# Layer 0 with both sequences sorted by expert, and layer 1's experts with their inner rows as 128 and 48, two blocks at a time

## The chip, the core and the metric

The kernel runs on one core of one Trainium2 chip. A core has a matrix engine (TensorE, PE in the profile, with its weight loads as PEld), a vector engine (VectorE, DVE), a scalar engine (ScalarE, ACT), a general engine (GpSimd, POOL) and SyncE (SP), which only issues transfers (DMA). Matrix results land in PSUM, which has eight banks of 128 x 512 floats; everything else lies in SBUF, in 128 partitions, or in the chip's main memory (DRAM in the code). The metric is the device time of one execution in microseconds, as the median of several runs. A profiled execution gives the trace that is read here.

## The reference

Two layers over x, 2 sequences of 1024 tokens with 128 floats each. Cut to what matters:

```python
for attn, ffn in ((L0_attn, L0_ffn), (L1_attn, L1_ffn)):
    xn = layernorm(x)
    x = x + attn(xn) + ffn(xn)

def L0_attn(x):      # 16 heads of 8, causal; q, k, v are x with signs
    return where(causal, sigmoid(4 * scale * q @ k.T), 0) @ v

def L0_ffn(x):       # 32 experts, inner width 64; each token takes 4
    cw = softmax(x @ gw + gb), kept for the best 4 in the best 4 of 8 groups
    y = sum over e of cw[:, e] * ((silu(x @ w1[e] + b1[e]) * (x @ w3[e] + b3[e])) @ w2[e] + b2[e])
    return y + (silu(x @ sw1 + sb1) * (x @ sw3 + sb3)) @ sw2 + sb2

def L1_attn(x):      # 16 heads of 8, softmax over all keys, with relative positions
    return softmax((q @ k.T + position term) * scale) @ v @ Wproj.T

def L1_ffn(x):       # 16 experts, inner width 176; each token takes 4; a shared expert of width 352
    w = sigmoid(x @ gate_w.T), the best 4 in the best 2 of 4 groups, normalised
    return sum over e of w[:, e] * ((silu(x @ gate[e].T) * (x @ up[e].T)) @ down[e].T) + shared(x)
```

## The kernel before, in words

**Order of work.** Only PE's order is written by hand: a table (`at(c, f, ...)`, L1319 on) says what is issued beside which attention step `c`, in three places of a step (before the scores, between scores and values, after the values), and a loop (L1444 to L1458) walks it. The other engines get their order from a scheduler that follows the program and the data; SP and POOL issue transfers in that order, one behind the other.

**Layer 0's attention** has 96 steps, 48 for each sequence (`steps0`, L714): one slice of four heads, one half of the queries (512), one tile of 128 keys. The order of the loops before is sequence, slice, half of the queries, key tile. `scores0` (L717) makes four matmuls (L731) into two double banks, two sigmoids on ACT (L737) and, where the key tile lies on the diagonal, a mask on POOL (L743). `values0` of the step before (L758) makes four more, into one bank that it adds up over the key tiles. Four of the eight key tiles of the second half, and all four of the first, lie on the diagonal, where the matmuls are 512, 384, 256 and 128 wide. Steps 0 to 47 are sequence 0.

**Layer 0's experts, sequence 0,** are dense: every token goes through all 32 experts. A unit is two experts (their inner widths of 64 side by side) and 512 tokens; `open_unit` issues two matmuls (L362, L363), a sigmoid (L375), two operations on DVE (L376, L377) and the weighting by the gate (L379, on POOL or DVE, with rows that L360 broadcasts by DMA), and `close_unit` adds one matmul (L391) into a bank. The 32 units are spread over steps 13 to 51 of the attention. The weights lie in SBUF whole (L116 to L121).

**Layer 0's experts, sequence 1,** are sorted. `gate0` (L449) picks four experts for each token, `counted0` (L537) counts with two matmuls, `sort0` (L547) works out on DVE in which slot each choice goes, so that each expert's tokens fill blocks of 128 slots, and `scatter0` (L611) writes the normalised rows to their slots by 32 indirect transfers on POOL. The 64 blocks are taken in quads: `fetch0` (L626) gets four blocks of rows and their weights through SP, `turn0` (L643) transposes them (L647), `hidden0` (L651) makes 16 matmuls (L659), `outputs0` (L669) four in two groups (L675) and stores the result. A quad is due every one and a half steps from step 57. Then `gather0` (L683) brings each token's four rows back, by 32 indirect transfers on POOL, and `gathered0` (L693) adds them on DVE. `clear0` (L427) fills the slots with zeros and `regroup0` (L416) writes the weights in the order that `fetch0` reads; both are DMAs alone. The shared expert of both sequences, and that of layer 1 (`blocks1`), go by units as well.

**Layer 1** scans maxima of the scores (L1184 on PE; L1204, L1209 on DVE) ahead of a softmax attention of 128 steps (L1245 scores, L1252 exponentials on ACT, L1264 values), and uses a buffer of relative positions (`rel`, L1139) up to the last of the transfers that spread them. At step 67 `experts` (L1007) stands in PE's order by itself: 79 blocks of 128 slots, of both sequences, sorted in the same way. `fetch_w` (L934) fetches one block's weights, 128 rows of `WX` = 608 floats (two halves of 88 columns of gate and of up, two of down with 40 rows of zeros), into a ring of six places; `fetch_x` (L951) fetches four blocks of rows; `turn_x` (L967) transposes them; `hidden` (L979) makes four matmuls for a block (L984), one sigmoid (L987) and two multiplications (L988, L989); `outputs` (L992) two matmuls for the block of two turns before (L999), and a store for every four blocks (L1003). Of the weights, four blocks are fetched ahead, two steps before the stage.

## Time and profile before

| what | us |
|---|---|
| median of 3 runs (1292.96 to 1298.01) | 1293.78 |
| the profiled execution | 1295.13 |
| its span in the trace | 1293.0 |
| first scores of sequence 0, layer 0 | 12.61 |
| first scores of sequence 1, layer 0 (step 48) | 226.14 |
| quads of sequence 1 | 254 to 361.8 |
| last values of layer 0's attention | 436 |
| first exponentials of layer 1 | 511 |
| layer 1's experts | 867.5 to 995.2 |

The mean granted clock of the core's PE was 0.956 of full speed. PE was busy for 1161.0 us of the span with 8781 matmuls, the DMA engines moved 204.77 MB. Where a row of the profile names a line, it is a line of the kernel as printed above; `out<-in` are the names of its tiles, the shape is partitions x elements (for PE: weights, then result), and behind a bar stand the busy time with the mean of one in ns, and then the engine's idle time just ahead of these instructions with what ended most of it. The row of digits called PEclk is the clock that PE was granted, in tenths, over 40 equal slices of the span; DMA is the mean busy share of the 16 DMA engines.

### The profile page before, as it was taken

The numbers are of one execution on the slowest core, as the hardware profiler recorded it, in microseconds if no ns is written. First come the engines' busy times: TensorE is split into PE (matmuls) and PEld (weight loads), VectorE is DVE, ScalarE is ACT, GpSimd is POOL, SyncE is SP. The second block draws the span as 40 slices with busy tenths as digits, with TensorE's granted clock in tenths as the row PEclk, the third lists the DMA queues.
The fourth block names the chain that finished last, engine by engine and source line by source line (L and its number), as shares of the span: only waits on it lengthen the run. The fifth ranks groups of instructions, "written<-read, shape, count | busy, mean of one in ns | idle before, by whom it ended". The sixth has DMA issues, their size and how long they took to land.

```text
span 1293.0 us, 24010 instructions
## 1 busy us (share of the span) xinstructions
PE 1161.0 (90%) x8781; PEld 577.1 (45%) x8781; DVE 782.9 (61%) x2420; ACT 613.0 (47%) x1102; POOL 370.4 (29%) x475
## 2 busy tenths in 40 slices
PE   5989899989989777897999999988999999998997
...
PEclk8999999998999867899999999999999999998998
DMA  6955843445233331363356645579996454563511
GB/s 186 238 152 156 259 126 110 133 128 149 85 93 122 111 106 49 98 196 99 125 170 211 208 138 169 188 229 281 288 287 201 138 185 158 174 216 120 174 50 29
DMA packets 196313, 204.77 MB, mean 158 GB/s; under 512 B 26436, under 2 KB 178244, under 8 KB 196196
## 3 DMA queue, kind: packets, MB, share of 16 engines
...
## 4 chain that ended last, share of the span: by engine, by line
PE 63%; DVE 19%; DMA 8%; issue 5%; ACT 3%; POOL 2%; SPq 0%; POOLq 0%; DVEq 0%; ACTq 0%
PE sm L1245 11%; PE sm L1184 8%; PE acc L1264 8%; PE sm L1235 5%; PE big L731 4%; PE acc L758 4%; PE sm L984 4%; DVE maxima L1209 3%; PE big L362 3%; DVE junk L1204 3%; PE sm L1135 3%; PE big L363 2%; DMA got<-slots_y,slot_of 2%; PE ffn L391 2%; DMA room<-wx 2%
## 5 line engine op out<-in xcount | busy, mean ns | idle before, releaser
L1252 ACT ACTIVATE p<-sm 128x512 f32<-128x512 f32 x512 | 264.8, 605 | 231.3 <-PE sm L1245 224.2
L1209 DVE TENSOR_REDUCE maxima<-sm 128x1 f32<-128x512 f32 (+3 forms) x472 | 226.8, 502 | 101.6 <-PE sm L1184 101.6
L737 ACT ACTIVATE at<-big 128x1024 f32<-128x1024 f32 (+1 forms) x192 | 144.9, 809 | 139.4 <-PE big L731 134.1
L1204 DVE CUSTOM_DVE_ANT_0 junk<-sm,near 128x384 f32<-128x384 f32 (+2 forms) x292 | 130.3, 446 | 64.3 <-PE sm L1184 63.9
L1264 PE MATMUL acc<-p,vs 128*32 128x512 f32 (+1 forms) x1288 | 145.2, 520 | 0.4 <-issue 0.4
L1235 PE MATMUL sm<-ident,near 128*128 128x128 f32 x704 | 109.8, 290 | 25.9 <-DVE maxima L1204 11.2
L731 PE MATMUL big<-qm,xT 32*128 32x512 f32 (+3 forms) x768 | 109.5, 556 | 7.6 <-DVE qm L724 3.8
L1235 PEld LDWEIGHTS sm<-ident,near 128*128 128x128 f32 x704 | 79.7, 145 | 80.5 <-ACT p L1252 35.4
L1245 PE MATMUL sm<-qa,kls 32*128 32x512 f32 (+3 forms) x832 | 112.3, 556 | 0.0
L1184 PE MATMUL sm<-kls,qs 32*128 32x512 f32 (+2 forms) x776 | 105.8, 572 | 6.7 <-POOL kls L1116 5.4
L910 POOL DMA_INDIRECT got<-slots_y,slot_of x64 | 64.9, 1014 | 163.1 <-ACT p L1252 152.6
L758 PE MATMUL acc<-at,xn 128*32 128x512 f32 (+3 forms) x768 | 86.8, 526 | 8.3 <-DVE attn L343 5.3
L743 POOL TENSOR_SCALAR_AFFINE_SELECT at<-at 128x512 f32<-128x512 f32 x64 | 41.8, 654 | 179.8 <-ACT at L737 175.9
L898 POOL DMA_INDIRECT slots_x<-xn,slot_of x64 | 62.4, 976 | 94.6 <-ACT p L1252 84.8
L1139 ACT COPY rel<-sm 128x512 f32<-128x512 f32 x112 | 57.5, 599 | 61.5 <-PE sm L1135 61.5
L920 POOL TENSOR_SCALAR got<-got,share 128x128 f32<-128x128 f32 x64 | 41.4, 646 | 113.4 <-DMA got<-slots_y,slot_of 113.0
L1264 PEld LDWEIGHTS acc<-p,vs 128*32 128x32 f32 x1288 | 26.5, 108 | 103.7 <-issue 94.8
L1184 PEld LDWEIGHTS sm<-kls,qs 32*128 32x128 f32 x776 | 36.5, 186 | 80.8 <-ACT p L1252 21.1
L731 PEld LDWEIGHTS big<-qm,xT 32*128 32x128 f32 x768 | 40.6, 190 | 66.3 <-issue 41.2
L1135 PE MATMUL sm<-posd,qs 32*128 32x256 f32 x448 | 58.1, 422 | 11.9 <-DVE maxima L1209 10.9
L1116 POOL TENSOR_SCALAR khs<-kf,not_aux,k_add 128x1024 f32<-128x1024 f32 x8 | 9.6, 1195 | 187.7 <-PE sm L1245 187.7
L1245 PE MATMUL sm<-qa,khs 32*128 32x512 f32 (+3 forms) x512 | 60.9, 509 | 0.0
...
## 6 DMA issues: line engine op xcount, KB each, us to landing
...
```

The lines of the kernel that those rows point to most:

```text
L731: nc.tensor.matmul(halves[r // 2][:, r % 2, off:TB], xT0[b][g, kt * P:(kt + 1) * P], masked[b, s][g, q * TB + off:(q + 1) * TB], start=Tru ...
L737: e = nc.scalar.activation(at[:, 2 * j:2 * j + 2, off:TB], sc[:, :, off:TB], AF.Sigmoid, scale=4.0 / math.sqrt(HD))
L758: nc.tensor.matmul(y[32 * r:32 * r + 32, off:TB], xn0[b][:, kt * P + 32 * r:kt * P + 32 * r + 32], at[:, r, off:TB], start=(kt == 0), stop ...
L910: d = nc.gpsimd.indirect_dma_start(y, None, slots_y[:, :], bass.IndirectOffsetOnAxis(ap=slot_of[:, t, j:j + 1], axis=0))
L1135: nc.tensor.matmul(ps[r][:, j, :], qs[g, t:t + P], posd[g, :], start=True, stop=True)
L1184: nc.tensor.matmul(ps[r][:, (k0 - lo) * P:(k1 - lo) * P], qs[g, qt * P:(qt + 1) * P], (kh if far else kl)[g, k0 * P:k1 * P], start=True, s ...
L1204: nc.vector.tensor_tensor_reduce(junk[:, 0:(k1 - k0) * P], part, near[n, i][:, r, w0:w0 + (k1 - k0) * P], 1.0, -BIG, ALU.add, ALU.max, mx[ ...
L1209: nc.vector.tensor_reduce(mx[:, r, slot:slot + 1], part, AX.X, ALU.max)
L1235: nc.tensor.matmul(ps[r][:, i * P:(i + 1) * P], near[n, i][:, r, w0:w0 + P], ident, is_transpose=True, start=(i == close[0]), stop=False, ...
L1245: nc.tensor.matmul(ps[r][:, i0 * P:i1 * P], k[g, kt * P:(kt + 1) * P], qa[n][g, i0 * P:i1 * P], start=(m == 0 and not close), stop=(m == l ...
L1252: e = nc.scalar.activation(p[:, r, :], ps[r], AF.Exp)
L1264: nc.tensor.matmul(y[rows_of(r), part], vs[:, kt, rows_of(r)], probs[n, kt][:, r, part], start=(kt == 0), stop=(kt == NT - 1 and part.stop ...
```

## The change

Layer 0: sequence 0 loses its dense units and takes the sorted way too, with the same functions (now with the sequence as an argument, called from a new function `way0`). `sort0` counts and ranks by 27 small matmuls for each sequence, into the `ffn` bank, in place of the additions on DVE. Within a quad the slots are numbered so that each partition's four rows lie side by side in memory (2 KB for a transfer instead of four times 512 bytes); the slot's number is worked out by bit operations. The attention's loops run sequence, half of the queries, slice, key tile. Sequence 0's scatters stand at steps 25 to 42 and its quads, one a step, at 47 to 62; sequence 1's scatters at 46 to 58 and its quads at 63 to 78; the gathers at 64 to 76 and 81 to 93. The weights of a quad have a ring of five, the rows one of three.

Layer 1: a block's weights are 128 rows of 496 floats (gate, the last 64 columns of up, the first 128 of up, the first 128 rows of down) and 48 rows of 128 floats (the rest of down) by a second transfer, which goes into the tile of the relative positions. A block takes three matmuls and two in place of four and two, and ACT and DVE work for two blocks at once (two sigmoids, four multiplications). The ring of weights has 12 places, of which eight are fetched one step before the stage. The rows of four blocks are laid out like the quads. Smaller: layernorm's iteration takes three operations instead of four; the second half of sequence 1's rows is turned for layer 1 behind the first scan instead of ahead of it; layer 1's shared units and the clears and regroups stand at other steps.

```diff
-I1H = I1 // 2
-WX = 4 * I1H + 2 * D
+I1R = I1 - P
+IU = I1 + I0
+WX = IU + P + D
...
-    w1, w3 = ([load(l0, f"{n}{i}", [P, E0 * I0 // 2], a[n][:, i * E0 * I0 // 2:(i + 1) * E0 * I0 // 2])
-               for i in range(2)] for n in ("w1", "w3"))
...
+        nc.vector.tensor_scalar(var[:, c], var[:, c], -0.5, None, ALU.mult)
         for _ in range(3):
             nc.vector.tensor_mul(t[:, c], rstd[:, c], rstd[:, c])
             nc.vector.tensor_mul(t[:, c], t[:, c], var[:, c])
-            nc.vector.tensor_scalar(t[:, c], t[:, c], -0.5, 1.5, ALU.mult, ALU.add)
-            nc.vector.tensor_mul(rstd[:, c], rstd[:, c], t[:, c])
+            nc.vector.scalar_tensor_tensor(rstd[:, c], t[:, c], 1.5, rstd[:, c], ALU.add, ALU.mult)
...
-        if b == 0:
-            rest = l0.tile([P, NT, E0 + 4], F32, tag="rest", name="rest")
-            nc.vector.memset(work[:, :, E0:], NOT)
-            yield from replaced4(work, best, rest)
-            cw = cw_of[b] = l0.tile([P, NT, E0], F32, tag="cw", name="cw")
-            nc.vector.scalar_tensor_tensor(cw, rest[:, :, 0:E0], GONE, sc, ALU.is_equal, ALU.mult)
-            return
...
+    def sort0(b):
+
+        ps = psum["ffn"].tile([P, TB], F32, tag="ffn", name="counts")
+        n_at = NT * E0
+        at = ps[:, 0:n_at]
         some = some0.rearrange("p t e -> p (t e)")
-        for i, m in enumerate((ahead, ones)):
-            nc.tensor.matmul(ps[:, i * NT * E0:(i + 1) * NT * E0], m, some, start=True, stop=True)
-        counted[b] = [l0.tile([P, NT, E0], F32, tag=n, name="counted") for n in ("sc", "work")]
-        for i, t in enumerate(counted[b]):
-            nc.vector.tensor_copy(t.rearrange("p t e -> p (t e)"), ps[:, i * NT * E0:(i + 1) * NT * E0])
-
-    def sort0(b):
-
+        col = l0.tile([E0, 2], F32, tag="sort_col", name="sort_col")
+        full = l0.tile([E0, NT], F32, tag="sort_full", name="sort_full")
+        n_blk = l0.tile([E0, 1], F32, tag="sort_blk", name="sort_blk")
+        wide = l0.tile([E0, P], F32, tag="work", name="sort_wide")
+        past = l0.tile([E0, NBLK0], F32, tag="sc", name="sort_past")
+
+        for t in range(NT):
+            nc.tensor.matmul(ps[0:E0, n_at:n_at + 1], some0[:, t, :], ones[:, 0:1], start=(t == 0), stop=(t == NT - 1))
+
+        nc.tensor.matmul(at, ahead, some, start=True, stop=False, skip_group_check=True)
+        for t in range(1, NT):
+            nc.tensor.matmul(at[:, t * E0:], ones, some[:, 0:n_at - t * E0], start=False, stop=False,
+                             skip_group_check=True)
+        nc.vector.tensor_copy(col[:, 0:1], ps[0:E0, n_at:n_at + 1])
+        nc.vector.tensor_scalar(full, filled[0:E0, 0:NT], col[:, 0:1], None, ALU.is_lt)
+        nc.vector.tensor_reduce(n_blk, full, AX.X, ALU.add)
+        nc.vector.tensor_scalar(wide, ones[0:E0, :], n_blk, None, ALU.mult)
         yield
-        rank, in_tile = counted[b]
-        at = l0.tile([P, NT, E0], F32, tag="rest", name="at0")
-        count = [l0.tile([P, E0], F32, tag=f"count{i}", name=f"count{i}") for i in range(4)]
-        n_tok, n_blk = count[0], count[1]
-        nc.vector.memset(at[:, 0, :], 0.0)
-        for t in range(1, NT):
-            nc.vector.tensor_add(at[:, t, :], at[:, t - 1, :], in_tile[:, t - 1, :])
-        nc.vector.tensor_add(n_tok, at[:, NT - 1, :], in_tile[:, NT - 1, :])
+
+        for t in range(NT):
+            nc.tensor.matmul(at[:, t * E0:(t + 1) * E0], wide, before, start=False, stop=(t == NT - 1),
+                             skip_group_check=True)
+        nc.tensor.matmul(ps[0:E0, n_at + 4:n_at + 5], upto, n_blk, start=True, stop=True)
+        nc.vector.tensor_copy(col[:, 1:2], ps[0:E0, n_at + 4:n_at + 5])
+        nc.vector.tensor_scalar(past, block_no[0:E0, 0:NBLK0], col[:, 1:2], None, ALU.is_ge)
         yield
-        nc.vector.tensor_add(at, at, rank)
-        full = some0.rearrange("p t e -> p (t e)").rearrange("p (e t) -> p e t", t=NT)
-        nc.vector.tensor_tensor(full, spread(n_tok, NT), filled[:, 0:NT].unsqueeze(1).to_broadcast([P, E0, NT]),
-                                ALU.is_gt)
-        nc.vector.tensor_reduce(n_blk, full, AX.X, ALU.add)
-        yield
-
-        end, d = n_blk, 1
-        while d < E0:
-            nxt = count[2 + (d in (2, 8))]
-            nc.vector.tensor_add(nxt[:, d:], end[:, d:], end[:, 0:E0 - d])
-            nc.vector.tensor_copy(nxt[:, 0:d], end[:, 0:d])
-            end, d = nxt, 2 * d
-        yield
-        first = count[0]
-        nc.vector.tensor_sub(first, end, n_blk)
-        nc.vector.tensor_scalar(first, first, float(P), None, ALU.mult)
-        nc.vector.tensor_tensor(at, at, first.unsqueeze(1).to_broadcast([P, NT, E0]), ALU.add)
-        yield
+        nc.tensor.matmul(ps[:, n_at + 8:n_at + 8 + NBLK0], ones[0:E0, :], past, start=True, stop=True)
         slot = l0.tile([P, NT, K0], F32, tag="slot0f", name="slot0f")
         for j in range(K0):
-            nc.vector.tensor_mul(some0, chosen0[j], at)
+            nc.vector.tensor_mul(some, chosen0[j].rearrange("p t e -> p (t e)"), at)
             nc.vector.tensor_reduce(slot[:, :, j], some0, AX.X, ALU.add)
-            yield
-        nc.vector.tensor_copy(slot0, slot)
+            if j % 2:
+                yield
...
+        s0, lo, hi = (l0.tile([P, NT, K0], U32, tag=n, name="slot0i") for n in ("index0", "drop", "best0"))
+        nc.vector.tensor_copy(s0, slot)
+        nc.vector.tensor_scalar(lo, s0, P - 1, 2, ALU.bitwise_and, ALU.logical_shift_left)
+        nc.vector.tensor_scalar(hi, s0, 7, 3, ALU.logical_shift_right, ALU.bitwise_and)
+        nc.vector.tensor_scalar(s0, s0, 9, 9, ALU.logical_shift_right, ALU.logical_shift_left)
+        nc.vector.tensor_tensor(lo, lo, hi, ALU.bitwise_or)
+        nc.vector.tensor_tensor(slot0[b], s0, lo, ALU.bitwise_or)
...
+        w = l0.tile([P, 4, 2 * P], F32, tag="bw0", name="bw0", bufs=5)
...
+        x = l0.tile([P, 4, P], F32, tag="bx0", name="bx0", bufs=3)
+        d = nc.sync.dma_start(x, of_quad(slots0_x[b], g))
...
+        x = (x2s[b] if (b, t // 4) in merged else xs[b])[:, t, :]
...
+        parts = [(P, sw1, sw3, sw2, sb1, sb3)]
...
-    steps0 = [(b, s, q, kt) for b in range(B) for s in range(NS) for q in range(NB)
+    steps0 = [(b, s, q, kt) for b in range(B) for q in range(NB) for s in range(NS)
               for kt in range(4 * (q + 1))]
...
+    def of_four(slots, g):
+        return slots[4 * g * P:4 * (g + 1) * P, :].rearrange("(p i) d -> p i d", p=P)
...
+        if i == 0:
+            nc.sync.dma_start(by_row[:, :, 0:I1], gate)
+        elif i == 1:
+            nc.sync.dma_start(by_row[:, :, I1:IU], up[:, :, I1 - I0:])
+            nc.sync.dma_start(by_row[:, :, IU:IU + P], up[:, :, 0:P])
+        elif i == 2:
+            nc.sync.dma_start(wx.rearrange("(e p) w -> e p w", p=P)[:, :, IU + P:], down[:, 0:P, :])
         else:
-            c = slice(2 * I1 + (i - 2) * D, 2 * I1 + (i - 1) * D)
-            nc.sync.dma_start(wx.rearrange("(e p) w -> e p w", p=P)[:, 0:I1H, c],
-                              a["dproj"].rearrange("(e j p) d -> j e p d", j=2, p=I1H)[i - 2])
-            nc.sync.dma_start(by_row[I1H:P, :, c], zeros[I1H:P].unsqueeze(1).to_broadcast([P - I1H, E1, D]))
+            nc.sync.dma_start(wd.rearrange("(e p) d -> e p d", p=P)[:, 0:I1R, :], down[:, P:, :])
...
+    RING = 12
...
+        k = i % RING
+        if k < 8:
+            if k % 2 == 0:
+                held[k // 2] = const.tile([P, T], F32, tag=("xn10", "xn11", "xT10", "xT11")[k // 2], name="blockw")
+            t = held[k // 2]
         else:
-            t = held["p"][i % 2][:, 0:T]
+            t = held["p"][k // 2 % 2]
+        t = t[:, k % 2 * WX:(k % 2 + 1) * WX]
...
+        row = first_row.pop(i)
+        nc.sync.dma_start(t, wx[bass.ds(row, P), :])
+        rest = held["rel"][I0:I0 + I1R, k * P:(k + 1) * P]
+        nc.sync.dma_start(rest, wd[bass.ds(row, I1R), :])
+        block_w[i] = t, rest
...
+    def hidden(j):
+
+
+        n = min(2, NBLK - 2 * j)
+        ps, ps2 = quads(small()), quads(small())[:, 0:n, :]
+        for k in range(n):
+            i = 2 * j + k
+            w, xT = block_w[i][0], block_xT[i // 4][:, i % 4, :]
+            for m in range(2):
+                nc.tensor.matmul(ps[:, 2 * m + k, :], w[:, m * IU:m * IU + P], xT, start=True, stop=True)
+            nc.tensor.matmul(ps2[0:I0 + I1R, k, :], w[:, P:IU], xT, start=True, stop=True)
+        h = pools["late"].tile([P, 2, P], F32, tag="bh", name="bh", bufs=3)[:, 0:n, :]
+        c = RING * P + 2 * P * (j % 4)
+        h2 = held["rel"][:, c:c + 2 * P].rearrange("p (k c) -> p k c", c=P)[:, 0:n, :]
+        g2, u2 = slice(0, I1R), slice(I0, I0 + I1R)
+        nc.scalar.activation(h, ps[:, 0:n, :], AF.Sigmoid)
+        nc.scalar.activation(h2[g2], ps2[g2], AF.Sigmoid)
+        nc.vector.tensor_mul(h, ps[:, 0:n, :], h)
+        nc.vector.tensor_mul(h, ps[:, 2:2 + n, :], h)
+        nc.vector.tensor_mul(h2[u2], ps2[g2], h2[g2])
+        nc.vector.tensor_mul(h2[u2], ps2[u2], h2[u2])
+        block_h[j] = h, h2[u2]
...
+            ps, (w, rest) = block_y[g][:, i % 4, :], block_w.pop(i)
+            nc.tensor.matmul(ps, h[:, k, :], w[:, IU + P:], start=True, stop=False)
+            nc.tensor.matmul(ps, h2[:, k, :], rest, start=False, stop=True)
...
+        for i in range(8, RING):
             fetch_w(i)
-        for i in range(NBLK + 2):
-            if i < NBLK:
-                hidden(i)
-            if i >= 2:
-                outputs(i - 2)
-                fetch_w(i + 4)
-            if i % 4 == 1:
-                turn_x(i // 4 + 1)
-                fetch_x(i // 4 + 2)
+        for j in range(N_PAIRS + 2):
+            if j < N_PAIRS:
+                hidden(j)
+            if j >= 2:
+                outputs(j - 2)
+                for k in range(2):
+                    fetch_w(2 * (j - 2) + RING + k)
+            if j % 2 == 0:
+                turn_x(j // 2 + 1)
+                fetch_x(j // 2 + 3)
...
+    def way0(b, gate, per, sort, scatter, rate, quads_at, back, back_rate):
+
+        every(gate, gate0(b), per)
+        order = sort0(b)
+        for c in (sort, sort + 2, sort + 3, sort + 4, sort + 4, sort + 5):
+            at(c, one_part, order, slot=MID)
+        at(sort + 7, biased0, b, slot=END)
+        for i in range(NT * K0):
+            at(scatter + int(i / rate), scatter0, b, i, slot=END)
+            at(back + int(i / back_rate), gather0, b, i, slot=END)
+            at(back + 2 + int(i / back_rate), gathered0, b, i, slot=END)
+        for g in range(NQ0):
+            c = quads_at + g
+            at(c, hidden0, b, g, slot=MID)
+            at(c + 1, outputs0, b, g, slot=END)
+            at(c - 1, turn0, b, g, slot=END)
+        for g in range(NQ0):
+            at(quads_at + g - 4, fetch0, b, g, slot=END)
...
+    FILL = 47
+    QUADS = FILL, FILL + NQ0
+    BACK = FILL + NQ0 + 1, FILL + 2 * NQ0 + 2
+    way0(0, 7, 1.25, 20, 25, 1.75, QUADS[0], BACK[0], 2.5)
+    at(26, normed0, 1, FIRST)
+    at(28, normed0, 1, LAST)
+    at(29, turned0, 1, (0,), slot=END)
+    at(30, turned0, 1, (1,), slot=END)
+    way0(1, 31, 1.5, 41, 46, 2.5, QUADS[1], BACK[1], 2.5)
...
-    for i in range(4):
-        beside(EXPERTS - 2, fetch_w, i)
+    for i in range(8):
+        beside(EXPERTS - 1, fetch_w, i)
...
```

## The prediction

> **What bounds the kernel now.** The page first: busy times, then the slices.
>
> ```profile
> PE 1161.0 (90%) x8781; PEld 577.1 (45%) x8781; DVE 782.9 (61%) x2420; ACT 613.0 (47%) x1102; POOL 370.4 (29%) x475
> ...
> PE   5989899989989777897999999988999999998997
> ...
> PEclk8999999998999867899999999999999999998998
> DMA  6955843445233331363356645579996454563511
> ```
>
> PE is busy nine tenths of the span in nearly every slice, and the DMA engines are full in one place, slices 27 to 29 (870 to 970 us), the stage of layer 1's experts. So PE work removed is time removed, if nothing it covered comes into the open, and the experts' stage is judged by itself. The busy times by stretch:
>
> ```profile
> 60.00:226.00 166.00, 153.79 (x761) 50.98 (x756) 94.08 (x223) 73.69 (x101) 62.76 (x65) 0.98 0.56 159
> 254.00:361.80 107.80, 100.19 (x826) 55.53 (x825) 59.86 (x205) 60.36 (x104) 10.64 (x16) 0.95 0.40 116
> 361.80:436.00 74.20, 62.69 (x355) 21.91 (x358) 33.55 (x84) 33.24 (x53) 36.74 (x42) 0.93 0.31 93
> 900.00:950.00 50.00, 47.90 (x425) 46.53 (x423) 27.14 (x66) 21.23 (x50) 0.00 (x0) 1.00 0.96 289
> ```
>
> Columns: stretch, length, busy PE, PEld, DVE, ACT and POOL, granted clock, DMA share, GB/s. Rows: sequence 0's layer-0 attention with its dense experts (PE 93%), sequence 1's quads, the rest of layer 0, the middle of layer 1's experts (PE 96%, but DMA 0.96 as well). The groups of what goes and comes:
>
> ```profile
> L362 PE MATMUL big<-xT,w 128*128 128x512 f32 x64 | 37.0, 660 | 12.9 <-DVE h L377 10.7 <-ACT at L737 2.0
> L363 PE MATMUL big<-xT,w 128*128 128x512 f32 x64 | 34.2, 617 | 0.0
> L391 PE MATMUL ffn<-h,w 128*128 128x512 f32 x64 | 36.5, 653 | 0.0
> L659 PE MATMUL hidden<-bxT,bw 128*64 128x128 f32 x256 | 19.2, 296 | 6.1 <-DVE bh L667 3.9 <-DVE bxT L649 2.2
> L675 PE MATMUL big<-bw,bh 128*128 128x256 f32 x64 | 19.0, 422 | 0.0
> L647 PE MATMUL big<-ident,bx 128*128 128x128 f32 x64 | 10.2, 282 | 0.0
> L614 POOL DMA_INDIRECT slots_x<-xn,slot x32 | 32.2, 1008 | 39.5 <-ACT at L737 35.5 <-issue 3.4 <-ACT sg L375 0.6
> ```
>
> **Layer 0, the PE sum.** Sequence 0's dense units go: 37.0 + 34.2 + 36.5 = 107.7 us of PE and the 12.9 us that PE waited in front of L362. Its 16 quads come, at sequence 1's price: 19.2 + 19.0 + 10.2 = 48.4 us, 3.0 a quad. Sorting on TensorE adds 27 small matmuls for each sequence; L647's 282 ns is the nearest row, so 2 x 27 x 0.28 = 15 us at most, 5 if most are narrow: 10. Net 120.6 - 58.4 = 62 us less, if no wait opens.
>
> **What the dense units covered.** In PE's timeline the attention's steps stand bare only before the units begin, at about 52 us:
>
> ```profile
> 25.80 2.09 PE L731 MATMUL big<-qm,xT 32*128 32x512 f32 x8 [2.40 <-DVE qm L724]
> 27.82 3.62 PE L335 MATMUL big<-gw,xT 128*128 128x32 f32 x16
> ...
> 42.91 0.93 PE L731 MATMUL big<-qm,xT 32*128 32x384 f32 x8
> 44.75 1.06 PE L758 MATMUL acc<-at,xn 128*32 128x512 f32 x8 [0.91 <-POOL at L743]
> 45.74 0.71 PE L731 MATMUL big<-qm,xT 32*128 32x256 f32 x8
> 46.39 0.85 PE L758 MATMUL acc<-at,xn 128*32 128x384 f32 x8
> 47.17 0.52 PE L731 MATMUL big<-qm,xT 32*128 32x128 f32 x8
> 48.45 0.64 PE L758 MATMUL acc<-at,xn 128*32 128x256 f32 x8 [0.76 <-POOL at L743]
> ```
>
> Columns: start, length, what, and in brackets the wait. A bare diagonal step waits for scores, two sigmoids and the mask on POOL, 0.76 to 0.91 us; inside the dense stretch (190 to 226 us) no such wait stands. I count one slice's steps with waits as 16.9 us for eight (the same timeline: five steps in 10.5 us, the other three at 2.1) against 14.2 of PE work; four short steps, which are all diagonal, as 7.8 against 5.9 (an estimate from ACT's and POOL's durations in the group).
>
> So, start to the end of sequence 0's attention: 12.6 us before the first scores + 13.2 (the first short group as it ran, at a low clock) + 3 x 7.8 + 4 x 16.9 = 117. Fill: two gates, transposes, two sorts, two shared units: 27. POOL: 32 scatters now fall at 1.75 per step; two stand 1.28 us apart in the trace of before, so 2.2 us a step plus masks, beside bare steps of 2.1: POOL gets late by some 7, and a late mask holds the values behind it on PE. Less 5 that fill takes up in waits: 146 us, against 226.1 where sequence 1's first scores stand now.
>
> Then 32 quads, one a step, instead of 16 over 24 steps. A step of PE work is 1.68 us (mean of four widths, scores and values), a quad 2.6 at full clock. Today's stretch 254 to 361.8 holds 16 x 2.6 + 24 x 1.68 + 8 = 90 of work in 107.8: factor 1.19. New: 32 x 2.6 + 31 x 1.68 + 7 = 142, x 1.19 = 169; to 315 us. The last steps (17 x 1.68, layer 1's projections, shared units: 61) at today's factor 74.2/59 = 1.25: 76, to 391. Today 436. Layer 0: **-45**; by the PE sum, 62 less some 17 of opened waits. Bounds: -58 (quad factor 1.10, no POOL lag) and -33 (1.28).
>
> **The clock, row against rule.** Removed filler can cost clock. Rows: behind the 2.40 us gap above, L731 took 2.09 instead of 1.07 and L335 3.62 instead of 1.96, about 10 us until the clock was back; behind gaps of 0.76 and 0.91 nothing slowed (1.06, 0.71). The Trainium skill, "TensorE: Matmul & The Clock Gate", section "Why this matters for your kernels", allows idle gaps up to about 3 us between bursts: by it the start would not have slowed at all; by the row a gap of 2.4 already costs, so a step that waits for a sort result or a late mask that long costs up to 10. I take the row, with one such drop within the 7 and the 27; by the rule layer 0 would be some 8 better.
>
> **Queues.** POOL is passed by 32 scatters and 32 gathers more, 64 x 1.28 = 82 us on 370; behind each wait masks, and behind these the values. In the quad stretch a step lasts 5 us, which holds 2.5 gathers, 3.2, and the mask: nothing is late. SP loses the broadcasts of L360 and gets 16 weight and 16 x loads: 1 MB per quad and 5.2 us is 200 GB/s with what clears run beside it, under the 289 seen. DVE loses L376 and L377 (23.9 us each in their groups) and half of L379 (11.3), and gets a second set of quads and a sort; it stays near 61%.
>
> **Layer 1's experts.** Now 867.5 to 995.2. Per block the chain shows L984 x8 in 0.88, L999 x4 in 0.45, 0.11 of others: 1.44 us, x 79 = 114; the remaining 14 are waits for weights and x:
>
> ```profile
> 909.21 4.88 DMA blockw<-wx
> ...
> 921.58 4.71 DMA room<-wx
> ```
>
> After: 3 + 2 matmuls in place of 4 + 2, so 0.66 + 0.45 + 0.11 = 1.22, x 79 = 96 for PE. ACT and DVE per pair of blocks stay below (2 x 0.38 and 4 x 0.42 against 2.4). The bytes: 253,952 + 24,576 of weights + 131,072 of x and y = 409,600 a block, x 79 = 32.4 MB, of which some 31.6 are left when PE begins: only block 0's weights and two groups of x come earlier, as the first rest shares the tile of the relative positions, waits for its last use, and the other seven blocks queue behind it on SP. SP issues 2.5 transfers a block, at 0.55 us each (its cadence before the stage) 1.36 x 79 = 107. Row against rule again: at share 0.96 the trace moved 289 GB/s, 109 us; "DMA: Bandwidth & Descriptors", "Specifications", gives about 358 GB/s for a core from HBM, 88 us, and PE would bind: -24. I take the row, plus 5 for the last two pairs: about 114, **-11** (the ring of 12 takes the waits that are jitter). Bounds -24 and 0 (two transfers a block cost more than the wider rows of x and y give).
>
> **At nearly nothing:** layernorm's three operations a step for four (2 us of DVE, under attention), the slot's bit operations and layer 1's sort (six of about 0.2 us, under the scans), clears and regroups moved (SP, no engine waits for it within 100 us); if that cover goes, 2 to 5 us, within the range. Between the layers, 436 to 511 now, one shared unit and the turn move behind the first scan: **-3** (-8 to +3).
>
> **Sum.** 1295.1 (the profiled execution) - 45 - 11 - 3 = 1236; the median of the runs is 1.3 lower: **1235**.
>
> **Rivals.**
> *A. Cover is dearer and the fetch does not shrink.* Masks waiting behind scatters on POOL and quads whose DVE chain (the 6.1 us in front of L659) paces a step: layer 0 gives 29 only, experts 2: 1262. For it: the factor 1.25 where little fills. Against: 16 quads ran at 1.19. 0.20.
> *B. DMA stops binding.* 2 KB runs for x and y (512 B now) and fewer bytes let PE bind at 96 + 5: -24; with -47 and -8 elsewhere: 1215; with layer 0's bound 1204. 0.14.
> *C. Slower: the clock.* Bare steps, with PE busy some 80%, are granted half clock throughout the first half. Then 108 us of PE work before the quads doubles, of which the waits take up 26: +82, 1317. The sign turns (+59) where 108/c - 108 - 26 = 59, at a mean clock c of 0.56 in the first 150 us. For it: the half clock from 23 to 37. Against: 1.00 in the stretch 40 to 60 us, half of it bare. 0.08.
> *D. Not felt:* A's causes at their worst, within 0.5%, about what a measurement of this kernel can tell from no change: 0.04.
> The forecast: 0.54. Range 1200 to 1268: A and B within, C and D out. Faster 0.88, same 0.04, slower 0.08.
>
> **What would show it.** Sequence 1's first scores near 146 us, last values near 391, quads about 5.2 us apart; waits on POOL's mask in the first 150 us of 0.7 to 1 us, clock over 0.9 there; the experts in about 114 us with DMA share still over 0.9 (if PE binds, B). Wrong if first-half gaps pass 2.4 us again and again, or the experts end on SP's issuing.

## The result, and the profile after

The change costs time. Over twelve runs each, the kernel before has a median of 1297.35 us (1292.96 to 1303.40), the changed kernel 1308.12 us (1301.21 to 1315.30): a ratio of 1.009, 95% interval 1.0067 to 1.0114, so 0.9% slower. The forecast was 1235 us, with a range that ended at 1268. The profiled execution took 1315.15 us (span 1313.5), 7 above its median; sums below are made against it. The two traces differ by 20 us, the medians by 11, so the misses below are together some 9 us too large.

Lines named from here on are those of the changed kernel, or of the run that is named, whose edits move them by a few. In the changed kernel L708 makes layer 0's scores, L735 its values and L720 the mask; L631, L643 and L659 are a quad's turns, hidden matmuls and outputs, L648 its sigmoids on ACT, L650 and L651 its two operations on DVE, L662 the copy of its outputs on ACT; L672 gathers a block of rows and L681 adds it to x.

The page's busy times and slices, in the form shown of before:

```profile
PE 1168.1 (89%) x8932; PEld 599.0 (46%) x8932; DVE 766.1 (58%) x2447; ACT 606.9 (46%) x1117; POOL 408.5 (31%) x521
...
PE   6897989997887878897999999969999999997997
...
PEclk9898899988986977798999999989999999997998
DMA  5969468855203341362455646478884455563511
```

PE is busy 7 us longer than before (1161.0), although it lost 107.7 us of dense units for quads that take 95.7 us where they took 48.4. The first 14 slices (to 460 us) are layer 0: the clock row shows 8 or less in seven of them, where before showed it in three, and PE's row has 7s and 8s to the end of layer 0. The 7s behind it stand where before has a 6, a 7 and an 8, and little time was lost there: from layer 1's first values to its experts 353.0 us, before 350.3.

The same by stretch (length; busy PE, PEld, DVE, ACT, POOL; granted clock, DMA share, GB/s): layer 0 up to sequence 1's first scores, the 32 quads, the rest of layer 0, and the middle of layer 1's experts.

```profile
12.00:168.00 156.00, 137.35 (x972) 54.44 (x972) 69.17 (x310) 81.17 (x108) 57.04 (x69) 0.88 0.76 211
168.00:354.00 186.00, 166.38 (x1296) 95.17 (x1295) 93.55 (x260) 86.05 (x158) 76.34 (x86) 0.93 0.61 187
354.00:447.00 93.00, 75.18 (x418) 28.80 (x414) 44.16 (x142) 41.16 (x61) 36.60 (x41) 0.85 0.26 80
...
900.00:950.00 50.00, 50.00 (x348) 42.62 (x348) 26.42 (x63) 18.25 (x47) 0.00 (x0) 1.00 0.82 244
```

In the last row PE is filled entirely, with 348 matmuls where the kernel before placed 425, while the DMA share fell from 0.96 to 0.82. Each matmul has become dearer. By marks that both traces have, the forecast missed here (layer 0 ends with its last values; the experts last from the first turn of their rows to the next scores of layer 1's attention):

| part | before | forecast | after | miss |
|---|---|---|---|---|
| start to sequence 1's first scores | | 146 | 168.0 | +22 |
| the quads, to the last outputs | | 169 | 187.1 | +18 |
| to layer 0's last values | | 76 | 92.1 | +16 |
| layer 0 in all | 436.3 | 391 | 447.2 | +56 |
| to the first x of layer 1's experts | 431.1 | 428 | 426.2 | -2 |
| experts | 128.6 | 117.6 | 138.9 | +21 |
| to the end of the span | 297.0 | 297 | 301.2 | +4 |

Layer 0's groups (0 to 447 us; busy, mean ns, then the idle time before them), the quads':

```profile
L643 PE MATMUL hidden<-bxT,bw 128*64 128x128 f32 x512 | 40.2, 306 | 7.5 <-DVE bh L651 5.5 <-DVE bxT L633 0.9 <-issue 0.8
L659 PE MATMUL big<-bw,bh 128*128 128x256 f32 x128 | 36.2, 405 | 0.0
L631 PE MATMUL big<-ident,bx 128*128 128x128 f32 x128 | 19.3, 273 | 0.0
```

(40.2 + 36.2 + 19.3) / 32 = 2.99 us a quad: priced right, and the waits in front of L643 sum to 7.5 us. So the time is not in the quads' own matmuls; it is in what stands around them. The attention's scores and values, the same matmuls in both kernels, have become dearer (from the two pages; before first, then after):

```profile
L731 PE MATMUL big<-qm,xT 32*128 32x512 f32 (+3 forms) x768 | 109.5, 556 | 7.6 <-DVE qm L724 3.8
L758 PE MATMUL acc<-at,xn 128*32 128x512 f32 (+3 forms) x768 | 86.8, 526 | 8.3 <-DVE attn L343 5.3
...
L708 PE MATMUL big<-qm,xT 32*128 32x512 f32 (+3 forms) x768 | 135.9, 589 | 20.2 <-ACT by L662 9.1
L735 PE MATMUL acc<-at,xn 128*32 128x512 f32 (+3 forms) x768 | 94.7, 569 | 25.0 <-POOL at L720 10.0
```

And DVE waits. Its list for 160 to 450 us (total, times, longest):

```profile
DVE x L681 <- DMA got<-slots_y,slot: 65.1, 37, 7.3
```

L681 adds a gathered row block onto x. In before the same operation waited half as long in this stretch, for one sequence instead of two:

```profile
DVE x L696 <- DMA got<-slots_y,slot: 30.5, 17, 6.1
```

In DVE's timeline (start, length, what, in brackets the wait before it) one such wait looks like this:

```profile
305.48 0.16 DVE L244 TENSOR_TENSOR ln_t<-ln_rstd 128x4 f32<-128x4 f32 x1
308.41 0.35 DVE L681 SCALAR_TENSOR_TENSOR x<-got,share,x 128x128 f32<-128x128 f32 x1 [2.77 <-DMA got<-slots_y,slot]
...
309.29 0.35 DVE L681 SCALAR_TENSOR_TENSOR x<-got,share,x 128x128 f32<-128x128 f32 x1 [0.26 <-DMA got<-slots_y,slot]
...
311.64 0.34 DVE L650 SCALAR_TENSOR_TENSOR bsg<-hidden,bias,bsg 128x128 f32<-128x128 f32 x1
312.02 0.35 DVE L651 SCALAR_TENSOR_TENSOR bh<-hidden,bias,bsg 128x128 f32<-128x128 f32 x1
```

And PE's timeline beside it:

```profile
313.66 1.97 PE L643 MATMUL hidden<-bxT,bw 128*64 128x128 f32 x16 [4.63 <-DVE bh L651]
315.56 1.94 PE L735 MATMUL acc<-at,xn 128*32 128x512 f32 x8
```

DVE stood from 305.6 to 308.4 for a row block of sequence 0, and a little later for another. Behind that addition in its queue stood the two operations that finish a quad of *sequence 1* (L650, L651). The sigmoid that L650 needs was done at 306.6; of the 5.0 us that passed until L650 began, 3.0 were this standing, the rest layernorm and an unloading ahead of it in the queue. PE waited 4.63 us, and its next two pieces of work took 1.97 and 1.94 us at a granted clock of 0.50. Until sequence 0's gathers begin, the first 18 spacings of quads sum to 87.9 us, 4.9 each; the remaining 13 to 96.4, 7.4 each.

### The profile page after: what moved, and what is told of

Read it like the earlier page. It is cut to its first block, busy times and chain, and to the rows that moved or that the text cites. A ratio compares the mean times of both kernels' runs of the same rounds, so it can differ in the third digit from the quotient of the medians.

```text
span 1313.5 us, 24765 instructions
## 1 busy us (share of the span) xinstructions
PE 1168.1 (89%) x8932; PEld 599.0 (46%) x8932; DVE 766.1 (58%) x2447; ACT 606.9 (46%) x1117; POOL 408.5 (31%) x521
## 4 chain that ended last, share of the span: by engine, by line
PE 63%; DVE 16%; issue 8%; DMA 5%; ACT 4%; POOL 3%; SPq 1%; another core or an unknown queue 0%; POOLq 0%; DVEq 0%; ACTq 0%
PE sm L1261 11%; PE sm L1200 9%; PE acc L1280 9%; PE sm L1251 6%; PE big L708 3%; PE sm L991 3%; PE sm L1151 3%; PE acc L735 3%; DVE maxima L1225 3%; PE sm L1014 2%; DMA got<-slots_y,slot 2%; DVE junk L1220 2%; PE sm L1013 2%; POOL got L672 2%; PE hidden L643 1%
## 5 line engine op out<-in xcount | busy, mean ns | idle before, releaser
L708 PE MATMUL big<-qm,xT 32*128 32x512 f32 (+3 forms) x768 | 135.9, 589 | 20.2 <-ACT by L662 9.1
L735 PE MATMUL acc<-at,xn 128*32 128x512 f32 (+3 forms) x768 | 94.7, 569 | 25.0 <-POOL at L720 10.0
L672 POOL DMA_INDIRECT got<-slots_y,slot x64 | 61.4, 959 | 101.6 <-ACT bsg L648 45.4
L708 PEld LDWEIGHTS big<-qm,xT 32*128 32x128 f32 x768 | 50.4, 201 | 85.9 <-issue 36.9
L600 POOL DMA_INDIRECT slots_x<-xn,slot x64 | 63.1, 985 | 49.9 <-ACT at L714 19.5
L720 POOL TENSOR_SCALAR_AFFINE_SELECT at<-at 128x512 f32<-128x512 f32 x64 | 41.7, 652 | 116.7 <-ACT at L714 111.5
```

The lines of the kernel that those rows point to most:

```text
L672: d = nc.gpsimd.indirect_dma_start(y, None, slots0_y[b][:, :], bass.IndirectOffsetOnAxis(ap=slot0[b][:, t, j:j + 1], axis=0))
L708: nc.tensor.matmul(halves[r // 2][:, r % 2, off:TB], xT0[b][g, kt * P:(kt + 1) * P], masked[b, s][g, off:TB], start=True, stop=True,)
L735: nc.tensor.matmul(y[32 * r:32 * r + 32, off:TB], xn0[b][:, kt * P + 32 * r:kt * P + 32 * r + 32], at[:, r, off:TB], start=(kt == 0), stop ...
```

## The experiments

The theory behind the runs has three parts: in layer 0, DVE's additions wait for gathered rows ahead of the quads' operations; in layer 1's experts, passes that alternate between 128 and 48 rows cost PE 0.42 us for two instead of 0.22; the clock lost in layer 0 is mostly a consequence. The rivals are masks behind gathers and scatters on POOL (the forecast's A), the clock as a cause by itself (C), the fetch of weights, and the gathers' pacing. All kernels start from the changed one. The marks are microseconds of the profiled execution, the ratio is to the kernel before, measured beside each run. Its medians there lie between 1291.5 and 1297.4 us, so runs are compared by their ratios where a few us matter.

| run | layer 0 ends | experts take | median | ratio [95%] |
|---|---|---|---|---|
| e1 | 448.8 | 126.2 | 1294.75 | 1.0027 [1.0004, 1.0049] |
| e2 | 447.0 | 125.7 | 1298.87 | 1.0056 [1.0026, 1.0086] |
| e3 | 428.5 | 138.4 | 1286.17 | 0.9948 [0.9925, 0.9972] |
| e4 | 445.5 | 138.7 | 1309.55 | 1.0142 [1.0114, 1.0171] |
| e5 | 452.0 | 138.6 | 1313.00 | 1.0109 [1.0074, 1.0144] |
| e6 | 441.4 | 138.7 | 1312.29 | 1.0134 [1.0094, 1.0174] |
| e7 | 443.8 | 127.8 | 1300.13 | 1.0029 [1.0012, 1.0045] |
| e8 | 444.0 | 126.4 | 1300.34 | 1.0026 [1.0001, 1.0052] |
| e9 | 444.1 | 107.9 | 1280.47 | 0.9871 [0.9843, 0.9900] |
| e10 | 463.6 | 138.9 | 1331.93 | 1.0240 [1.0192, 1.0287] |
| e11 | 466.6 | 109.1 | 1303.73 | 1.0053 [1.0023, 1.0083] |
| e12 | 461.5 | 108.7 | 1304.25 | 1.0057 [1.0038, 1.0076] |
| e13 | 403.2 | 108.4 | 1233.56 | 0.9575 [0.9531, 0.9618] |
| e14 | 458.1 | 107.2 | 1291.59 | 0.9986 [0.9960, 1.0012] |
| e15 | 431.6 | 107.9 | 1266.91 | 0.9828 [0.9774, 0.9881] |
| e16 | 422.9 | 138.4 | 1284.42 | 0.9949 [0.9928, 0.9971] |
| e17 | 413.1 | 110.3 | 1236.83 | 0.9576 [0.9546, 0.9605] |
| e18 | 402.5 | 108.7 | 1237.50 | 0.9572 [0.9497, 0.9647] |

**e1: layer 0's change alone.** Layer 1's experts, with their sort and fetches, are those of before.

```diff
-        for j in range(N_PAIRS + 2):
+        for i in range(NBLK + 2):
```

> Layer 0 as changed, layer 1's experts, their sort and their fetches as before. Theory: both halves of the change lost something. The changed trace has layer 0 ending 11 us later (447 against 436), the stretch to the first exponentials 6 us shorter, and the experts' stage 137.0 us instead of 127.6; so this kernel should lie 0 to 6 us above before (1297 to 1303) and its experts' stage at 126 to 129 us. Rival: layer 1's part did bring its 11 us and layer 0 alone costs 20 or more: then 1318 or more.

Layer 0 ends at 448.8, as late as in the changed kernel. So the lost gain of layer 0 belongs to layer 0's own edits, and the experts' edits cost the rest.

**e2: the 48-row passes made into 112 rows.** The rows above the 48 hold zeros in the weights, so the result is unchanged.

```diff
+            nc.gpsimd.memset(held["rel"][0:I0, 0:(RING + 8) * P], 0.0)
-        block_w[i] = t, rest
+        block_w[i] = t, held["rel"][0:I0 + I1R, k * P:(k + 1) * P]
-        block_h[j] = h, h2[u2]
+        block_h[j] = h, h2[0:I0 + I1R]
```

> The matmul of the 48 rest rows is made over rows 0 to 111, with zeros in weights 0 to 63; nothing is fetched more. Theory: in the changed trace the pair of outputs, 128 rows and then 48, takes 0.42 us for two passes where two passes of 128 rows take 0.22, so a block takes 1.60 us instead of 1.22; with 112 rows this goes, a block comes down to about 1.25, and the stage from 137 to 108 (PE) or 116 us (if the fetch of 31.6 MB then binds): total 1281 to 1290. Rival: the second transfer of each block paces the stage through SP and the DMA engines, PE's passes only fill the wait: then the stage stays over 130 us and the total within 4 us of the changed kernel.

PE's timeline of the experts, changed kernel (start, length, what):

```profile
898.86 0.39 PE L1013 MATMUL sm<-blockw,bh 128*128 128x128 f32 x2
899.18 0.48 PE L1014 MATMUL sm<-room 48*128 48x128 f32 x2
899.59 0.49 PE L1013 MATMUL sm<-blockw,bh 128*128 128x128 f32 x2
900.01 0.49 PE L1014 MATMUL sm<-room 48*128 48x128 f32 x2
```

and with 112 rows (e2):

```profile
902.30 0.39 PE L1014 MATMUL sm<-blockw,bh 128*128 128x128 f32 x2
902.52 0.39 PE L1015 MATMUL sm<-room 112*128 112x128 f32 x2
902.74 0.39 PE L1014 MATMUL sm<-blockw,bh 128*128 128x128 f32 x2
902.97 0.39 PE L1015 MATMUL sm<-room 112*128 112x128 f32 x2
```

Read the starts: two passes of 128 rows and two of 48 follow each other at 0.32 to 0.42 us a line, of 128 and 112 at 0.22. Smaller matmuls had become the dearer ones, and padding them with zeros takes 13 us off the stage (138.9 to 125.7). The edit changes two things at once, the number of rows and the partition at which they begin (64 for the 48 rows, 0 for the 112); which of them counts, no run parts. The gain stops there, 8 us above the forecast. SP's queue in the same stage of e2 shows the next bound:

```profile
906.43 0.33 SPq L966 DMA_DIRECT2D room<-slots_x  x1
906.88 0.35 SPq L1020 DMA_DIRECT2D slots_y<-by  x1
907.49 0.34 SPq L954 DMA_DIRECT2D blockw<-wx  x1
908.03 0.34 SPq L956 DMA_DIRECT2D room<-wd  x1
908.55 0.34 SPq L954 DMA_DIRECT2D blockw<-wx  x1
...
911.77 0.33 SPq L956 DMA_DIRECT2D room<-wd  x1
912.21 0.37 SPq L966 DMA_DIRECT2D room<-slots_x  x1
```

The whole round of four blocks, ten transfers, takes 912.21 - 906.43 = 5.78 us, 0.58 each; 79 blocks make 114 us. That is SP issuing back to back.

**e7: e2 with the first eight rests fetched last**, behind x, against a wait of 6.62 us in e2 (7.37 in the changed kernel) for the first weights at the stage's start.

```diff
+    for i in range(8):
+        beside(EXPERTS - 1, fetch_rest, i)
```

> As e2_rest_112_rows, and the rests of the first eight blocks are fetched behind the eight blocks' weights and the first rows instead of each with its weights. Theory: the 6.6 to 7.4 us in front of the second pair of hidden matmuls is SP's queue, which stands at the first rest until the tile of the relative positions is free; without it the weights are there: no wait over 2 us at the stage's start, its start to end 125.7 us becomes 117 to 120, as it is otherwise held by the fetch. Rival: the weights' own transfers are late because the DMA engines are full then: the wait stays over 5 us.

The longest wait at the start falls to 4.30 us, and the stage takes 127.8: nothing over e2. The recorded theory (117 to 120) missed, which fits a stage that is set by its issuing as a whole.

**e9: e2 with the 48-row rests issued by POOL.**

```diff
-        nc.sync.dma_start(rest, wd[bass.ds(row, I1R), :])
+        nc.gpsimd.dma_start(rest, wd[bass.ds(row, I1R), :])
```

> As e2_rest_112_rows, and the rests are fetched by POOL's queue instead of SP's. Theory: with the slow passes gone, SP's issuing binds the stage: in e2 ten transfers for four blocks go out in 5.85 us, 0.585 us each, at a DMA share of 0.89; with six on SP (3.5 us for four blocks) PE (1.25 us a block, 99 us) or the DMA engines (32.4 MB at 289 GB/s, 112 us) bind, and the stage from turning the first rows to its end goes from 125.7 to 105 to 116 us. Rival: the DMA engines already bind at 273 GB/s, as two short transfers cost more than their bytes: then 122 us or more.

The stage falls from 125.7 to 107.9 us. The middle of the stage in e9, with the columns as above:

```profile
900.00:950.00 50.00, 49.80 (x449) 49.61 (x448) 33.51 (x80) 21.94 (x57) 20.66 (x41) 1.00 0.97 325
```

449 matmuls fill PE where e2 placed 369 and the changed kernel 348; the DMA engines move 325 GB/s where before showed 289 at a share of 0.96, and e2 273. So SP's issuing was the bound of e2, and 289 is no limit of the DMA engines for these transfers. Before moved the rows of x and y in pieces of 512 B, not of 2 KB; whether 289 was the limit for those, no run tests.

**e4: idle filled.** Extra matmuls keep PE busy in the bare steps of the first 150 us.

```diff
+        if 6 <= c <= 16 or 29 <= c <= 32 or 37 <= c <= 40:
+            ps = psum["ffn"].tile([P, TB], F32, tag="ffn", name="idle")
+            nc.tensor.matmul(ps[:, 0:2 * P], ident, xT0[0][:, 0:2 * P], start=True, stop=True)
```

> Added: 19 matmuls of 128x128 by 256 columns (about 0.5 us each) whose result nobody reads, each ahead of the values that wait for a mask, in steps 6 to 16, 29 to 32 and 37 to 40. Theory: what sequence 0's first half lost is clock, behind waits of 0.8 to 2.5 us: granted clock in 12 to 168 us was 0.88; with the waits filled it is 0.94 or more, and the 156 us stretch gets no longer, or up to 6 us shorter, although 9.5 us of work are added. Rival: the clock follows something else (narrow matmuls, the temperature of the day): clock as now, and the stretch 5 to 9 us longer.

From 58 to 168 us the changed kernel and e4 show, in this order:

```profile
58.00:168.00 110.00, 99.15 (x700) 41.28 (x696) 37.30 (x149) 57.14 (x72) 46.56 (x53) 0.88 0.71 200
```

```profile
58.00:168.00 110.00, 101.16 (x755) 42.82 (x752) 39.77 (x152) 59.47 (x75) 48.73 (x55) 0.95 0.72 205
```

The clock rises from 0.88 to 0.95; the first quad starts at 160.4 instead of 164.4, where the other kernels with this front part scatter from 156 to 168; the total does not gain. The clock can be bought back here, but it is worth no more than the scatter.

**e5: the masks of steps 24 to 47 on DVE instead of POOL**, which tests masks waiting behind scatters.

```diff
+            if kt * P >= q * TB and 24 <= i < 48:
+                nc.vector.tensor_mul(at[:, :, off:off + P], at[:, :, off:off + P], tri.unsqueeze(1).to_broadcast([P, NG, P]))
```

> The masks of sequence 0's steps 28 to 47 are made on DVE, as a multiplication by a triangle of ones, not on POOL, where sequence 0's scatters stand in steps 25 to 42. Theory: a mask waits on POOL behind scatters of 0.97 us each, the values behind it on PE; in the changed trace that is 5.4 us of waits in 60 to 160 us, 4.1 of them from 122 to 129 us, and behind them half clock up to 140 us, some 8 us more; so the first quad's hidden matmuls (164.4 us) come 8 to 13 us earlier. Rival: a mask on DVE is as late, behind the gate of sequence 1 that stands there: then within 3 us.

PE's waits for POOL's mask (5.9 us from 60 to 168 us in the changed kernel) are gone; waits for ACT (2.5) and DVE (1.9) stand in their place, and the quads start at 164.2. A bare step has a wait, whichever engine makes the mask.

**e3: sequence 0's additions left out.** Its gathered rows are fetched but not added, so sequence 0's x lacks its layer-0 experts.

```diff
+            if b:
                 at(back + 2 + int(i / back_rate), gathered0, b, i, slot=END)
```

> Left out: the addition of sequence 0's gathered rows on DVE (its routed experts' share of the result); scatters, quads and gathers stay. Theory: in the changed trace DVE stands 65 us for gathered rows between 160 and 450 us, with the quads' own operations queued behind, and PE waits for these and falls to half clock behind each wait; without sequence 0's adds the stretch of the quads (168 to 354 us, 186) takes 168 to 175, the total is 10 to 20 us lower. Rival: the quads are paced by the three double banks of PSUM and ACT's copies that free them (9.1 us of waits in nine places): then no more than 4 us.

Layer 0 ends 19 us earlier; the last 13 spacings of the quads fall from 96.4 to 74.6 us. The first 18 do not fall. This is the additions' price in the quad stretch.

**e6: additions two steps later, with more buffers; e8: e6 and e7.**

```diff
-        x = l0.tile([P, 4, P], F32, tag="bx0", name="bx0", bufs=3)
+        x = l0.tile([P, 4, P], F32, tag="bx0", name="bx0", bufs=2)
-        y = moe.tile([P, D], F32, tag="got0", name="got0", bufs=6)
+        y = moe.tile([P, D], F32, tag="got0", name="got0", bufs=10)
-            at(back + 2 + int(i / back_rate), gathered0, b, i, slot=END)
+            at(back + 4 + int(i / back_rate), gathered0, b, i, slot=END)
```

> The additions of gathered rows stand four steps behind their gathers, not two, with ten buffers for the rows instead of six; the quads' rows have two places instead of three. Nothing is left out. Theory: DVE's waits for gathered rows (65 us from 160 to 450 us) fall to under 25 us, and a good part of the 19 us by which layer 0 ended earlier without sequence 0's additions comes: last values at 432 to 440 us, total 7 to 15 us under the changed kernel. Rival: the additions keep their place in DVE's order ahead of the rows' landing, since the gathers themselves are paced and limited by buffers: then no gain, within 3 us.

> The edits of e6_adds_later and e7_rests_last together. Theory: they lie in different stages and add up: 20 to 35 us under the changed kernel, that is 1275 to 1288 where the kernel before has 1297, and faster than both. Rival: what layer 0 gains is waited for again in layer 1: then no more than the better of the two.

Both in fact leave something out: three of the four additions of sequence 1's fourth token tile now come after layer 1's normalization has read x. The edit missed its aim: the waits for rows come to 75.6 us, not fewer, because the order in which the instructions were queued kept the additions where they had been. e8 adds e6 to e7 and gains nothing over it. Neither run speaks for or against the theory.

**e10: gathers not paced; e11: e9 and e10; e12: e11 and e4.** If the rows come too late because their gathers are issued late, issue them as early as they can be.

```diff
-        paced(d)
```

> The gathers of layer 0 are no longer tied to the last sigmoid that was issued ahead of them (an order that the kernel adds, no need of the data); nothing is left out. Theory: DVE's waits for rows make a ring with that order: a quad's sigmoid on ACT releases the gathers on POOL, these land some 2 us behind their issue, DVE adds them ahead of the next quad's operations, and so the next sigmoid is late; with the gathers free to go as soon as buffers allow, DVE's waits for rows fall from 65 us to under 35, and the last values come 8 to 18 us earlier than 447. Rival: six buffers and the 1.28 us between gathers hold the ring as well: then within 4 us.

> The edits of e9_rests_on_pool and e10_gathers_unpaced together. Theory: they add up, 25 to 40 us under the changed kernel: 1268 to 1283 where that has 1308 and the kernel before 1297. Rival: as in e9 and e10, each for its own part.

> e11_both with e4's 19 unread matmuls. Theory: in e4 they brought the first quad 4 us earlier, and this was lost again behind the gathers; with the gathers free, 3 to 5 us under e11. Rival: the end of layer 0 follows the quads' own pace: equal to e11 within 2 us.

DVE's waits for rows do fall, from 65.1 to 29.5 us, and layer 0 still ends 16 us later. The gathers now go out in two bunches, mostly one every 1.26 us, and the additions come in bunches with them, still ahead of other work. While those of sequence 0 run (to 302 us), three spacings of the quads are 16.2, 16.7 and 12.0 us; soon after they are 4.4 to 4.9. Those of sequence 1 start at 363.61 us, nearly each with a wait for its gather. The sigmoid of a shared unit was done at 365.6 us, but its two operations on DVE (L374, L375) began 18.6 us later, behind the additions, and PE stood until the second was done (DVE's timeline of e10, then PE's):

```profile
382.54 0.35 DVE L680 SCALAR_TENSOR_TENSOR x<-got,share,x 128x128 f32<-128x128 f32 x1 [0.79 <-DMA got<-slots_y,slot]
...
384.23 0.75 DVE L374 SCALAR_TENSOR_TENSOR t<-big,sb,sg 128x512 f32<-128x512 f32 x1
...
385.68 0.75 DVE L375 SCALAR_TENSOR_TENSOR h<-big,sb,t 128x512 f32<-128x512 f32 x1
```

```profile
386.48 1.12 PE L258 MATMUL big<-ident,xn 128*128 128x128 f32 x4 [19.59 <-issue]
```

So the pacing was not the fault: without it the same fault stands in other places. e11 keeps e9's gain in the experts and e10's loss in layer 0; e12 takes the time of e11, so the idle filler does nothing there either.

**e13: e9, and sequence 0's additions queued behind a quad's last operation on DVE.** The dependency orders the queue only; no semaphore is added.

```diff
+            last_h["name"] = nc.vector.scalar_tensor_tensor(
+                quad_h[b, g][:, j, :], ps[:, 1, j, :], bb, sg[:, j, :], ALU.add, ALU.mult).ins.name
...
+        if b == 0:
+            tc.add_manual_dep(d.ins, last_h["name"], mybir.DependencyInfo(
+                mybir.DependencyClass.Sync, mybir.DependencyReason.SCHED_ONLY), reason="behind the quad")
```

> As e9_rests_on_pool, and each addition of a gathered row of sequence 0 is put behind the quad's last multiplication on DVE that was issued ahead of it; nothing is left out, gathers and their pace stay. Theory: what e3 gained (19 us in layer 0) was the place of the additions in DVE's order, ahead of a quad whose rows wait on PE, not the additions' own 11 us; so DVE's waits for rows fall from 65 us to under 45, and layer 0's last values come 6 to 15 us earlier than e9's 444; total 1266 to 1275. Rival: the place changes nothing, e3 gained by fewer operations on DVE: within 3 us of e9's 1280.

The largest step of the study: 1233.56 us, 47 under e9 by the medians and 38 by the ratios. Layer 0 ends at 403.2 instead of e9's 444.1. DVE's waits from 160 to 450 us in e13:

```profile
DVE bsg L650 <- ACT bsg L648: 44.0, 46, 2.5
DVE x L682 <- DMA got<-slots_y,slot: 29.6, 17, 4.9
```

and a piece of its timeline:

```profile
292.62 0.69 DVE L633 COPY bxT<-big 128x512 f32<-128x512 f32 x1 [0.71 <-PE big L631]
293.23 1.11 DVE L682 SCALAR_TENSOR_TENSOR x<-got,share,x 128x128 f32<-128x128 f32 x3
...
295.98 0.35 DVE L650 SCALAR_TENSOR_TENSOR bsg<-hidden,bias,bsg 128x128 f32<-128x128 f32 x1 [1.63 <-ACT bsg L648]
```

Three additions run together without a wait, in a gap where DVE would have stood for PE and ACT anyway. In the stretch of the quads the wait for rows has become a wait for a sigmoid that the quad needs anyway; the 29.6 us that are left lie behind the quads.

**e14: e9, and the quads' turns in another group of banks; e15: e13 and e14.** This tests whether scores wait for the banks that the turns hold.

```diff
-        ps = quads(small())
+        ps = quads(psum["ffn"].tile([P, TB], F32, tag="ffn", name="turned"))
```

> As e9_rests_on_pool, and the quads' transposed rows go through the single bank of the hidden matmuls, not through one of the three double banks. Theory: a step takes four double banks (two scores, a turn, an output) of three, and scores wait for the copy that frees one (9.1 us in nine places, and more inside the scores' own busy time); with three of three these waits go, 5 to 10 us. Rival: the turn then waits for the quad before to be read out of the single bank by DVE: as long as now or up to 15 us longer.

> The edits of e13 and e14 together. Theory: both are waits of the quads' steps, so they add up only in part: 8 to 20 us under e9. Rival: the worse of the two decides.

Each is slower than its base, by 11 us (1291.59 against 1280.47; 15 by the ratios) and by 33 (1266.91 against 1233.56). The recorded rival came: from 158 to 366 us e14's PE waits no more for the copies that free the scores' banks (15.9 us in e9), but 41.8 us in front of the turns. So the scores gain nothing from this exchange; what more banks for both would do is not tested.

**e16: the changed kernel with e13's order of additions alone.**

> The changed kernel with nothing but e13's order: each addition of sequence 0's gathered rows behind the quad's last multiplication on DVE. Theory: layer 0 and layer 1's experts lose by themselves; e13 lies 47 us under e9 (1233.6 against 1280.5), so this lies 40 to 50 us under the changed kernel, 1258 to 1268, with the experts' stage at 137 to 140 us as there. Rival: part of e13's gain needed POOL's and SP's other load of e9: then over 1275.

1284.42 us: the additions' order alone is worth 24 us by the medians, 18 by the ratios (0.9949 against 1.0090), and turns the change from a loss into a gain of 0.5%. The last 13 spacings of the quads sum to 75.4 us, as in e3 (74.6), which has no additions: the order takes away their whole price in the quad stretch. From sequence 1's first scores to the last outputs it is 166.4 us, where 169 were forecast. But layer 0 ends 20 us later than in e13, and the expectation of 1258 to 1268 missed; its rival (over 1275, as e9's other load was needed) gave the number, but hardly the cause: e17 below has that load too and runs this stretch as slowly.

**e17: e13 with sequence 1's additions also behind ready work on DVE. e18: e13 once more, unchanged, on another chip.**

```diff
-        if b == 0:
-            tc.add_manual_dep(d.ins, last_h["name"], mybir.DependencyInfo(
+        if True:
+            tc.add_manual_dep(d.ins, (last_d if b else last_h)["name"], mybir.DependencyInfo(
```

Here `last_d` is the last operation on DVE that unloads values or finishes a shared unit.

> As e13_adds_behind_quad, and the additions of sequence 1's gathered rows are put behind the last unloading of values or the last shared unit's multiplication on DVE that was issued ahead of them. Theory: in e13 DVE still stands 30 us for rows, behind the quads, with PE waiting 7.5 us for an unloading and 6.5 for a shared unit; with the order, the last 17 attention steps (313 to 403 us) take 78 to 85 us instead of 90, total 3 to 12 us under e13. Rival: there the additions end the path themselves, as layer 1's normalization needs them: no gain, or some us lost.

> The kernel of e13 once more, unchanged, to see whether its even quads are its own. In e13's profile the last outputs stand at 312.9 us and the first 18 quads are 4.5 us apart; e16 and e17, with the same order on DVE in that stretch, have 329.6 and 332.1 and 5.2 us. Theory: this is scatter from execution to execution (buffers that come free a little later, behind SP's queue): the last outputs lie at 320 to 335 here, the total within 10 us of 1234. Rival: it belongs to the program: 313 again within 4 us.

In e17 the stretch from the last outputs to the last values takes 81 us (332.1 to 413.1) where e13 takes 90 and the changed kernel 92; the waits for rows fall to 10.9. The total is that of e13, because the quads, in a stretch that the edit does not touch, took 171.5 us from the first hidden matmul to the last outputs instead of 154.8. e18 repeats e13: last outputs at 311.0, against 312.9. It was expected to show scatter, and did not; so the even quads belong to the program, not to a chip.

**What stays open.** Compare the quad stretch of e13 and e16:

```profile
158.00:313.00 155.00, 151.93 (x1332) 93.13 (x1336) 92.54 (x248) 86.94 (x163) 80.08 (x91) 0.99 0.73 230
```

```profile
159.60:329.60 170.00, 159.27 (x1332) 94.00 (x1333) 91.67 (x246) 87.31 (x163) 79.94 (x91) 0.97 0.67 209
```

The same 1332 matmuls, and up to the end of layer 0 the same order of instructions on all five engines; PE stands 3.1 us in the one and 10.7 in the other. From 158 to 240 us, before any addition of sequence 0, e16's scores wait 3.3 us for ACT's copies of quads' outputs (L663), e13's never. The two part at 172 us, at a quad's sigmoid on ACT (e13, then e16):

```profile
169.49 0.37 ACT L648 ACTIVATE bsg<-hidden,bias 128x128 f32<-128x128 f32 x1
...
172.41 0.37 ACT L648 ACTIVATE bsg<-hidden,bias 128x128 f32<-128x128 f32 x1 [1.32 <-remote]
```

PE's rows before it are alike, 1.49 us later in e16, but there the sigmoid stood 1.32 us for a signal whose sender the profile does not show ("remote"), and the copy and the scores behind it came later by that. The changed kernel has the same wait (1.33 us, at 177.3). What held the signal back was not found. So 18 to 24 us of e13's gain over e9 are explained by the additions; some 20 more are measured and unexplained.

## Why the prediction was wrong, step by step

**The PE sum** had the amount of work right and its price wrong. A quad was to cost 3.0 us and cost 2.99; the sorts take 13.1 us where 10 was taken. By the sum PE's busy time in layer 0 was to fall by 49 us (107.7 - 58.4) and its idle time to grow by 4 (17 of opened waits, less the 12.9 in front of L362). Busy time fell from 387.1 to 380.4, by 7, and idle time grew from 48.9 to 66.6, by 18. So of the 56 us by which layer 0 missed, 43 are a PE that is busy longer and 14 are waits. 34 of the 43 are the scores and values, which the forecast took at the price of full clock (1.68 us a step): 135.9 + 94.7 against 109.5 + 86.8.

**The clock** is at most 27 us of this. Length times (1 - clock) over layer 0's stretches is 214 x 0.04 + 136 x 0.04 + 74 x 0.07 = 19 us before, and 156 x 0.12 + 186 x 0.07 + 93 x 0.15 = 46 after; it is an upper bound, as idle time at low clock is in it. The forecast had "one such drop", 10 us at most, within the 7 and the 27; there were many. PE's timeline (wait in brackets) in the first stretch:

```profile
125.62 0.85 PE L735 MATMUL acc<-at,xn 128*32 128x384 f32 x8 [2.50 <-POOL at L720]
...
128.83 1.08 PE L735 MATMUL acc<-at,xn 128*32 128x256 f32 x8 [1.61 <-POOL at L720]
129.84 2.09 PE L708 MATMUL big<-qm,xT 32*128 32x512 f32 x8
```

After gaps of 2.50 and 1.61 us, scores took 2.09 instead of 1.07, and the granted clock (third figure from the end) was half:

```profile
126.40:140.00 13.60, 11.99 (x74) 7.05 (x70) 1.28 (x2) 4.64 (x6) 7.58 (x9) 0.50 0.53 139
```

Elsewhere gaps of 1.15 (at 82.34) and 0.81 us (at 108.02) were followed by values of 1.94 and 1.74, but one of 1.29 us (at 121.22) by 1.06, so the length of one gap does not decide. The Trainium skill's rule ("TensorE: Matmul & The Clock Gate", "Why this matters for your kernels": gaps up to about 3 us) would have been even further off than the row of 2.4 us that was used. But e4 shows that the clock is mostly a follower in this stretch: filled back to 0.95, it gained at most the 4 us of the first quad's start.

**The start to 168 us (+22).** 137.35 us busy at 0.88 holds some 120 of work. By an estimate from these numbers that is the forecast's 81 of steps (48 x 1.68) and 39 of fill instead of 27 (12 us), with 16 to 19 of clock loss where some 7 to 10 were allowed. POOL's late masks (rival A's first half) were in the sum, and e5 shows that moving them gains nothing.

**The quad stretch (+18): the step that failed.** The forecast named the queues of POOL and SP, found that "nothing is late", and of DVE said only that it "stays near 61%". A share says nothing about order. The additions of gathered rows stand in DVE's queue ahead of the quads' own operations, and with 32 quads in a row there is always a quad behind them: 96.4 us for 13 spacings instead of 75.4 (e16, whose whole stretch meets the forecast). Rival A's mark was right (a DVE chain paces the quads), its cause was not: it is not the length of the chain but an instruction of another sequence, waiting for a DMA in front of it.

**The last steps (+16).** The factor of 1.25 from before was exceeded in the main for the same reason: sequence 1's additions wait, and the values' unloading on DVE behind them. e17, which orders them, takes 81 us where e13 takes 90 and 76 were forecast.

**The experts (+21).** "0.66 + 0.45 + 0.11" took a block's outputs at the price of before, where four passes of 88 rows each follow each other in 0.45 us, 0.22 a pair. In alternation of 128 rows with 48 a pair takes 0.32 to 0.42; padded (e2), it takes 0.22 again and the stage is at 125.7. The second term that failed is SP: "1.36 x 79 = 107" was computed, and set aside as it lay under the DMA bound of 109. At the measured 0.58 us each it is 114 and comes first. And the DMA bound did not hold for the new transfers: with SP relieved (e9) the stage took 107.9 at 325 GB/s. The forecast chose the row (289) over the figure of the Trainium skill ("DMA: Bandwidth & Descriptors", "Specifications", about 358); what came out lies midway between the two.

**Between the layers** -3 was forecast; -5 came up to the experts' first x, as -8 between the layers and +3 in layer 1's attention. Rival B (PE binds the experts) is what e9 makes true, with PE busy for 49.80 of 50 us; rival C (half clock throughout) did not happen: the lowest stretch is 0.85.

Two sums of the forecast do not come out as written, without changing its outcome: 114 us for the experts is 14 under today's 127.7, not 11, and the bound of -58 (quad factor 1.10, no POOL lag) comes to -65.
